# Gathering a tile's two entries one by one instead of together, in a four-layer graph kernel

## The chip, the cores and the metric

The kernel runs on one core of one Trainium2 chip. Its time is device time in microseconds (us) of one execution, as the median of the runs shown. The core has five engines, each with its own stream of instructions: TensorE (PE; its weight loads stand as PEld), VectorE (DVE), ScalarE (ACT), GpSimd (POOL) and SyncE (SP). [...]

## The reference

There are 16 entries. Each has 1024 nodes with 64 features and a dense adjacency of 1024 x 1024. Four layers follow each other, each added to its input and normalised over the features:

```
x = layernorm(x + gnn0(x, adj))     # two small matmuls on [x, adj @ x], tanh between them
x = layernorm(x + adj @ x / degree)
x = layernorm(x + quantile_gnn(x, adj, W1, b1, W2, b2))
x = layernorm(x + quantile_gnn(x, adj, W1', b1', W2', b2'))

def quantile_gnn(x, adj, ...):
    # drop some neighbours by their rank, keep the diagonal: the same set for both layers
    # per node and feature: sort the features of the neighbours that are left
    # agg = 0.25 * q(0.25) + 0.5 * q(0.5) + 0.25 * q(0.75), with linear interpolation
    return relu((x + agg) @ W1 + b1) @ W2 + b2
```

The last two layers cost the most: for each of 16 x 1024 nodes, and for each of 64 features, some 8 to 33 values are sorted, and that twice.

## The kernel before

**Tiles.** In each entry the nodes are ordered by their number of neighbours and cut into eight tiles of 128 nodes. The seven tiles of nodes with fewest neighbours (t = 0 to 6) have lists of 10, 11, 13, 14, 15, 17 and 19 slots (`SIZES`). Slot 0 is the node itself, the other slots hold its neighbours. The eighth tile is treated apart: TensorE picks its rows with one-hot matrices (`fill`, L762).

**Rounds.** Two entries, 2p and 2p + 1, are sorted together, as member m = 0 and m = 1 of a pair. A round is one pair in one of the two quantile layers. `order_of_rounds` (L953) alternates the layers after two rounds of the first; the first round of all has its two members sorted one after the other instead of together. `tasks` (L957) lists all tiles of all rounds, from t = 6 down to t = 0 in each.

**The ring.** The neighbours' rows come from tables in DRAM (six for each layer, one entry in each, L352) into a ring in SBUF, `got_s` (L1070): 60 slots (`ROOM`) for each of the two members. `fetch` (L977) gives a task the next free slots. For each member it has ScalarE copy slot 0 (L997), and GpSimd gather one slot after the other with an indirect DMA (L378, called at L999): one gather fetches one row of 64 floats for each of 128 nodes. A gather needs three things: the list of rows (`idx`, made by VectorE at the end of `lists`, L502), the table (written at L495 for the first layer, and at L888 by eight indirect DMAs for the second), and the slot free of its earlier user.

Tiles 6, 5 and 4 take 19 + 17 + 15 = 51 of the 60 slots. Tile 3 needs 14 and doesn't fit behind them, so it begins again at slot 0, once tile 6 is through.

**The sort.** `sort_round` (L1022) calls `fetch(n)` for each task, sorts by pairwise minimum and maximum on VectorE (`exchange`, L1014), and leaves the weighting of the sorted slots to `weigh` (L811), on ScalarE (L829) and VectorE. While a task's comparisons are written, `fetch()` is called after each one, and looks ahead.

**The order of the work.** All other work of the kernel (layers 0 and 1, lists, matmuls behind the sort, the eighth tile) consists of Python generators that `Weave` (L908) interleaves with the sorts. It decides by the estimated VectorE time that has been written so far. For VectorE, ScalarE and TensorE this written order is the order in which they run, because L1065 sets `manual_schedule` for these three. GpSimd and SyncE aren't in that list: the order of their streams is decided afterwards by the tile framework's scheduler, which puts each instruction where it finds it ready. So `fetch` fixes what a gather depends on and where slot 0's copy stands on ScalarE, and the scheduler fixes where the gather stands on GpSimd.

**SyncE** loads adjacency blocks (L433), writes the first layer's tables (L495) and reads the second layer's features back from DRAM (`read_back`, L902). `ready(b)` (L973) tells that an entry's lists and first-layer features have been written.

Of the kernel before, what the change touches and what calls it, by code (L numbers as in the profile page):

```python
# [25 lines left out]
SIZES = (10, 11, 13, 14, 15, 17, 19, 21, 33)  # L26
# [3 lines left out]
LINKS = [sum(SIZES[:t]) - t for t in range(LISTED + 1)]  # L30
KW = max(SIZES)
WIDE = max(2 * max(SIZES[:LISTED]), KW)
TABLES = 6
HOTS = 6
ROOM = 60
# [181 lines left out]
def adj_resnorm_kernel(ctx: ExitStack, tc: tile.TileContext, x, adj_t, nodemask, w01, b01, w02, b02,  # L217
                       w21, b21, w22, b22, w31, b31, w32, b32, out):
    nc = tc.nc
# [102 lines left out]
    for t, want in enumerate(wants):  # L322
        for first, m, stride, length in regular_runs(want):
            for r in range(m):
                k = first + r * stride
# [26 lines left out]
    table = [[dram.tile([N + 1, C], F32, name=f"table{layer}{i}") for i in range(TABLES)] for layer in range(2)]  # L352
# [24 lines left out]
    def gather(dst, tab, rows):  # L377
        nc.gpsimd.indirect_dma_start(out=dst, out_offset=None, in_=tab,  # L378
                                     in_offset=bass.IndirectOffsetOnAxis(ap=rows, axis=0))
# [377 lines left out]
    def members(k):  # L757

        layer, pair = order_of_rounds[k]
        return layer, [(m, 2 * pair + m, entries[2 * pair + m]) for m in range(2)]  # L760
# [188 lines left out]
    weave = Weave()  # L949
    tails = {}  # L950
    free, gots, room, holders = set(), [], [0], [None] * ROOM
    allowed = [1]
    order_of_rounds = [(0, 0), (0, 1)]  # L953
    for pair in range(2, B // 2):
        order_of_rounds += [(1, pair - 2), (0, pair)]
# [1 line left out]
    tasks = []  # L957
# [15 lines left out]
    def ready(b):  # L973

        return entries[b].listed and entries[b].xs[0] is not None

    def fetch(must=-1):  # L977

        while len(gots) < len(tasks):
            n = len(gots)  # L980
            k, t, present = tasks[n]
            layer, both = members(k)
            first = room[0] if room[0] + SIZES[t] <= ROOM else 0
            taken = [i for i in holders[first : first + SIZES[t]] if i is not None and tasks[i] not in free]
            there = [e.xs[1] is not None if layer else ready(b) for m, b, e in both if m in present]
            if n > must and (taken or not all(there)):
                return
            assert not taken
            holders[first : first + SIZES[t]] = [n] * SIZES[t]
            room[0] = first + SIZES[t]  # L990
            got = ring[:, :, first : first + SIZES[t], :]
            for m, b, e in both:
                if m not in present:
                    continue
                while not (e.xs[1] is not None if layer else ready(b)):
                    weave.advance()
                nc.scalar.copy(got[:, m, 0, :], e.xs[layer][:, t, :])  # L997
                for i in range(1, SIZES[t]):
                    gather(got[:, m, i, :], table[layer][b % TABLES], e.idx[:, LINKS[t] + i - 1 : LINKS[t] + i])  # L999
            gots.append(got)  # L1000

    def finish_round(k, agg, sums):
        for gen in sums:
# [10 lines left out]
    def exchange(t, pair, view):  # L1014

        for is_max, d, v, i, j, to in usual[t]:
            dve.tensor_tensor(view(pair[to], v, d if is_max else 0), view(pair[i], v), view(pair[j], v, d),
                              op=ALU.max if is_max else ALU.min)
            weave.catch_up()
            fetch()  # L1020

    def sort_round(k):  # L1022
# [13 lines left out]
        for n, (_, t, present) in enumerate(tasks):  # L1036
            if tasks[n][0] != k:
                continue
            fetch(n)
            got = gots[n]  # L1040
            which = slice(present[0], present[-1] + 1)
            count = len(present)
            other = s.lists.tile([P, WIDE, C], F32, name="other", bufs=1)
            other = other[:, : count * SIZES[t], :].rearrange("p (e s) c -> p e s c", e=count)
            exchange(t, (got[:, which], other), cut_pair)
            summed(t, got, which, present)
# [11 lines left out]
    with ExitStack() as main:  # L1058
# [11 lines left out]
        ring = s.lists.tile([P, 2, ROOM, C], F32, name="got_s")  # L1070
# [294 lines left out]
```

## Time and profile before

| what | value |
|---|---|
| time, median of 3 runs | 5304.49 us (5294.7 to 5307.4) |
| the profiled execution, its own time | 5293.2 us |
| span of that execution, first to last instruction | 5291.5 us |
| mean granted TensorE clock | 0.745 of full speed |

| engine | busy us | share of the span | instructions |
|---|---|---|---|
| PE (matmul) | 3412.4 | 64% | 43576 |
| DVE | 4296.5 | 81% | 9266 |
| ACT | 2809.6 | 53% | 6314 |
| POOL | 3467.3 | 66% | 3296 |

How to read it: a group of instructions is told by its line, engine, operation and tiles (what is written <- what is read), how many there were, their busy time, the mean duration of one in ns, and the idle time of the engine just before them with what ended most of it. "issue" is time in which an engine waited for nothing that the profile shows. [...]

### The profile page before, as it was taken

How to read it: one execution, taken by the hardware profiler on the slowest of the kernel's cores; microseconds unless marked ns; L12 is line 12 of the kernel's file. 1: busy time of each engine (PE TensorE's matmuls, PEld its weight loads, DVE VectorE, ACT ScalarE, POOL GpSimd, SP SyncE). 2: the span in 40 equal slices, each digit the busy share in tenths (PEclk: the TensorE clock that was granted, in tenths of full speed). 3: DMA queues.
4: the chain of work that ended last, by engine and by line, in shares of the span. 5: the costliest groups of instructions: out<-in, count | busy, mean ns of one | idle time of the engine just before them, and what ended most of it. 6: DMA issues, size and time to landing. Idle time of an engine off the chain costs nothing. (4 is left out here: it accounts for less than half of the span.)

```text
span 5291.5 us, 109614 instructions
## 1 busy us (share of the span) xinstructions
PE 3412.4 (64%) x43576; PEld 2637.1 (50%) x43576; DVE 4296.5 (81%) x9266; ACT 2809.6 (53%) x6314; POOL 3467.3 (66%) x3296
## 2 busy tenths in 40 slices
PE   6887886385765786766686775777769563424152
PEld 5656665263553665555564553655557352324141
DVE  2577848798788989897987987799899999596775
ACT  3566465466564665737383663738475653323242
POOL 0435327757477776767677674776767777777771
PEclk7888786697877787878687786877878775555555
DMA  2212212122222222221212122221212111111110
GB/s 84 79 50 72 65 39 59 46 52 53 52 54 52 59 62 57 57 57 45 70 43 57 50 48 53 57 59 50 60 51 58 25 28 26 26 24 27 26 24 7
DMA packets 420618, 259.31 MB, mean 49 GB/s; under 512 B 106603, under 2 KB 368891, under 8 KB 420091
## 3 DMA queue, kind: packets, MB, share of 16 engines
q1 hardware_dynamic: 317690, 147.12, 9.7%
q0 software_dynamic: 102400, 105.06, 9.4%
q8 instruction: 343, 5.62, 0.4%
q14 instruction: 185, 1.51, 0.1%
HBM read 239.37 MB, written 12.59 MB: 48 GB/s over the span
## 5 line engine op out<-in xcount | busy, mean ns | idle before, releaser
L378 POOL DMA_INDIRECT got_s<-table,idx x2944 | 3172.8, 1078 | 1634.3 <-issue 594.8
L374 PEld LDWEIGHTS <-hot 128*128 128x128 bf16 x24576 | 960.1, 108 | 1024.5 <-DVE hot L211 704.3
L374 PE MATMUL pgk<-x3p,hot 128*128 128x64 bf16 x12288 | 540.1, 210 | 469.6 <-DVE hot L211 402.9
L211 DVE TENSOR_TENSOR other<-got_s 128x512 f32<-128x512 f32 (+9 forms) x850 | 508.2, 609 | 390.7 <-DMA got_s<-table,idx 363.2
L374 PE MATMUL pgk<-x2p,hot 128*128 128x64 bf16 x12288 | 517.5, 207 | 321.2 <-DVE hot L211 258.9
L780 ACT COPY got<-pgk 64x256 f32<-64x256 f32 x416 | 151.9, 365 | 670.3 <-PE pgk L374 667.0
L211 DVE TENSOR_TENSOR got_s<-got_s 128x128 f32<-128x128 f32 (+9 forms) x867 | 481.9, 559 | 19.5 <-ACT got_s L829 1.7
L536 PE MATMUL pr<-steps,near 128*128 128x512 bf16 x1536 | 412.7, 429 | 131.6 <-ACT junk L542 83.5
L481 PE MATMUL pa<-x,adj_r 128*128 128x65 f32 x2048 | 387.6, 372 | 135.0 <-ACT x L404 58.1
L628 PE MATMUL pk<-near,order 128*128 128x512 f16 x2048 | 466.5, 381 | 3.9 <-DVE order L211 3.8
L829 ACT ACTIVATE got_s<-got_s,wts 128x64 f32<-128x64 f32 x1568 | 396.7, 336 | 135.4 <-DVE got_s L211 129.4
L481 PEld LDWEIGHTS pa<-x,adj_r 128*128 128x128 f32 x2048 | 377.2, 287 | 142.8 <-ACT x L404 60.1
L211 DVE TENSOR_TENSOR got_s<-other 128x512 f32<-128x512 f32 (+9 forms) x731 | 402.0, 563 | 7.5
L211 DVE TENSOR_SCALAR hot<-place 128x1024 bf16<-128x1024 f16 x768 | 329.1, 434 | 56.5 <-PE pgk L374 56.5
L211 DVE TENSOR_TENSOR other<-other 128x384 f32<-128x384 f32 (+10 forms) x617 | 323.7, 525 | 17.3
L536 PEld LDWEIGHTS <-near 128*128 128x128 f16 x1536 | 161.5, 108 | 351.8 <-issue 225.8
L211 DVE MAX8 best<-code 128x8 f16<-128x1024 f16 x240 | 293.8, 1224 | 45.9 <-ACT code L639 40.8
L628 PEld LDWEIGHTS <-order 128*128 128x128 bf16 x2048 | 193.9, 98 | 232.6 <-issue 11.6
L542 ACT ACTIVATE junk<-pr,nb_st 128x1024 f16<-128x1024 f32 x256 | 281.9, 1106 | 35.6 <-PE pr L536 34.9
L790 ACT ACTIVATE hot<-far,one_f 128x1024 bf16<-128x1024 f16 x256 | 294.0, 1148 | 8.4
L788 ACT ACTIVATE far<-place,minus_k 128x1024 f16<-128x1024 f16 x256 | 292.8, 1144 | 6.2 <-DVE place L211 4.4
L580 PE MATMUL pv<-minus_n,takes 128*128 128x128 bf16 x1024 | 209.5, 239 | 132.6 <-DVE takes L211 132.1
(205 smaller groups left out, 6727.9 us busy)
## 6 DMA issues: line engine op xcount, KB each, us to landing
adj_r<-in_adj_dram SPq DMA_DIRECT2D x256, 512.0 KB
got_s<-table,idx POOLq DMA_INDIRECT x2944
x_s<-in_x_dram SPq DMA_DIRECT2D x16, 256.0 KB
table<-x SPq DMA_DIRECT2D x16, 256.0 KB
x<-table SPq DMA_DIRECT2D x16, 256.0 KB
table<-x3s,rows POOLq DMA_INDIRECT x128
out_dram<-agg,out_rows POOLq DMA_INDIRECT x128
table<-no_row SPq DMA_DIRECT2D x12, 0.2 KB
```

Source lines behind the costliest of these rows:

```text
L211: return call(*args, **kwargs)
L374: nc.tensor.matmul(dst, hot[:, c, :], parts[:, c, q, :], start=first and c + q == 0, stop=c == NT - 1 and q == 2)
L378: nc.gpsimd.indirect_dma_start(out=dst, out_offset=None, in_=tab, in_offset=bass.IndirectOffsetOnAxis(ap=rows, axis=0))
L481: nc.tensor.matmul(pa[:, q, :], adj[i][:, jt, :], x1[:, jt, :], start=jt == 0, stop=jt == NT - 1)
L536: nc.tensor.matmul(pr[:, h * HALF : (h + 1) * HALF], near[:, c, t * P : (t + 1) * P], steps[:, ONSET + h * HALF - c * P :][:, :HALF], star ...
L542: nc.scalar.activation(junk, prs[t - 1], AF.Sign, bias=lim[:, i, t - 1 : t], scale=-1.0, accum_out=cut_at[:, i, t - 1 : t])
L580: nc.tensor.matmul(pv[:, cols], takes[:, c, rows], minus_n, start=False, stop=False)
L628: nc.tensor.matmul(cols, order[:, c, t * P : (t + 1) * P], left(c, slice(h * G, (h + 1) * G)), start=c == 0, stop=c == NT - 1)
L780: nc.scalar.copy(got[rows, off + waiting[0] : off + waiting[0] + 4, :], waiting[1][rows])
L788: nc.scalar.activation(far, e.place, AF.Abs, bias=minus_k[:, i + 2 : i + 3])
L790: nc.scalar.activation(by_act, far, AF.Relu, bias=one_f, scale=-1.0)
L829: nc.scalar.activation(got[:, m, i, :], got[:, m, slot_id, :], AF.Copy, scale=e.wts[:, t, i : i + 1])
```

## The change

`fetch` keeps one place for each member (`fetched`) in the list of tasks, in place of one for both. A new function, `fetch_one`, handles one member of one task. Member 0 may go ahead of member 1; member 1 may not pass member 0. The member that comes to a task first takes the ring slots for both. Before, a task was begun only once both members' lists had been written and the slots were free; after, each member begins once its own lists have been written and the slots are free. What is gathered, into which slots and from which lists, stays the same, and so do the copies of slot 0.

```diff
-    allowed = [1]
+    allowed, fetched = [1], [0, 0]
...
     def fetch(must=-1):
 
-        while len(gots) < len(tasks):
-            n = len(gots)
-            k, t, present = tasks[n]
+        moved = True
+        while moved:
+            moved = False
+            for m in range(2):
+                n = fetched[m]
+                if n < len(tasks) and (m == 0 or n <= fetched[0]):
+                    moved = fetch_one(n, m, must) or moved
+
+    def fetch_one(n, m, must):
+
+        k, t, present = tasks[n]
+        if m in present:
             layer, both = members(k)
-            first = room[0] if room[0] + SIZES[t] <= ROOM else 0
-            taken = [i for i in holders[first : first + SIZES[t]] if i is not None and tasks[i] not in free]
-            there = [e.xs[1] is not None if layer else ready(b) for m, b, e in both if m in present]
-            if n > must and (taken or not all(there)):
-                return
-            assert not taken
-            holders[first : first + SIZES[t]] = [n] * SIZES[t]
-            room[0] = first + SIZES[t]
-            got = ring[:, :, first : first + SIZES[t], :]
-            for m, b, e in both:
-                if m not in present:
-                    continue
-                while not (e.xs[1] is not None if layer else ready(b)):
-                    weave.advance()
-                nc.scalar.copy(got[:, m, 0, :], e.xs[layer][:, t, :])
-                for i in range(1, SIZES[t]):
-                    gather(got[:, m, i, :], table[layer][b % TABLES], e.idx[:, LINKS[t] + i - 1 : LINKS[t] + i])
-            gots.append(got)
+            _, b, e = both[m]
+
+            def there():
+                return e.xs[1] is not None if layer else ready(b)
+
+            if n > must and not there():
+                return False
+            if n == len(gots):
+                first = room[0] if room[0] + SIZES[t] <= ROOM else 0
+                if any(i is not None and tasks[i] not in free for i in holders[first : first + SIZES[t]]):
+                    assert n > must
+                    return False
+                holders[first : first + SIZES[t]] = [n] * SIZES[t]
+                room[0] = first + SIZES[t]
+                gots.append(ring[:, :, first : first + SIZES[t], :])
+            while not there():
+                weave.advance()
+            got = gots[n]
+            nc.scalar.copy(got[:, m, 0, :], e.xs[layer][:, t, :])
+            for i in range(1, SIZES[t]):
+                gather(got[:, m, i, :], table[layer][b % TABLES], e.idx[:, LINKS[t] + i - 1 : LINKS[t] + i])
+        elif n >= len(gots):
+            return False
+        fetched[m] = n + 1
+        return True
```

## The prediction

> **What bounds the kernel now.** I read the page's busy times and costliest groups first, then the waits of each engine, then GpSimd's work around one start of a round. From the page:
>
> ```profile
> PE 3412.4 (64%) x43576; PEld 2637.1 (50%) x43576; DVE 4296.5 (81%) x9266; ACT 2809.6 (53%) x6314; POOL 3467.3 (66%) x3296
> L378 POOL DMA_INDIRECT got_s<-table,idx x2944 | 3172.8, 1078 | 1634.3 <-issue 594.8
> ```
>
> VectorE is the bound: 4296.5 of 5291.5 us, in a stream that runs in written order. The other 995 us are waits or start-up. GpSimd is second, with 2944 gathers. From the views of the waits of VectorE, GpSimd and ScalarE:
>
> ```profile
> DVE other L211 <- DMA got_s<-table,idx: 363.2, 29, 26.4
> ...
> DVE other L211 <- ACT got_s L997: 9.8, 4, 5.2
> ```
> ```profile
> POOL got_s L378 <- DVE idx L211: 305.4, 6, 177.3
> ...
> POOL got_s L378 <- DVE y_x L211: 125.0, 5, 123.8
> ```
> ```profile
> ACT got_s L997 <- DVE agg L211: 23.8, 4, 12.7
> ```
>
> (Total, times, longest.) The largest single wait of VectorE is for gathers, 363.2 us in 29 pieces, and GpSimd stood idle 305.4 us for lists. So gathers that start earlier would be worth something. The question is whether the change makes them start earlier.
>
> The start of the second round (entries 2 and 3) answers it. GpSimd's timeline there:
>
> ```profile
> 568.56 1.00 POOL L378 DMA_INDIRECT got_s<-table,idx  x1 [43.34 <-DVE idx L211]
> ...
> 630.46 0.94 POOL L378 DMA_INDIRECT got_s<-table,idx  x1 [0.30 <-issue]
> 755.16 0.95 POOL L378 DMA_INDIRECT got_s<-table,idx  x1 [123.75 <-DVE y_x L211]
> ```
>
> and the instructions on the ring in three stretches (length; then DVE, ACT, POOL busy, with counts):
>
> ```profile
> 568.00:630.00 62.00, 0.00 (x0) 0.00 (x0) 47.42 (x47) 0.73 0.34 84
> 631.50:755.00 123.50, 0.00 (x0) 0.23 (x1) 0.00 (x0) 0.85 0.09 27
> 755.00:816.00 61.00, 15.62 (x24) 0.81 (x5) 47.13 (x46) 0.89 0.24 61
> ```
>
> From 568.56 to 630.46 a gather starts every 1.25 us, which makes 48. One member's share of tiles 6, 5 and 4 is 18 + 16 + 14 = 48, all that fits in the ring. Then GpSimd stops for 123.75 us, until the next member has its table and lists. The order of the two built programs, which holds no times, names the tables; both have:
>
> ```
> L378 DMACopy got_s<-table02 (entry 2) x48
> L378 DMACopy got_s<-table03 (entry 3) x48
> ```
>
> So member 0 is already gathered alone, before member 1's lists exist, in the kernel before. Python writes these gathers late, but GpSimd's stream isn't in written order: the scheduler moves each gather forward to where its inputs are ready. The wait for "both" that the change takes away stands in the Python code and not on the chip.
>
> **What the Trainium skill says.** "Perfetto Trace Analysis", section "Sequencer Loop": an engine's instructions are queued in order, and each waits for its own semaphores. So only a changed place in a stream, or a changed semaphore, can change the time, and I count these two. "DMA: Bandwidth & Descriptors", section "Anatomy of one DMA — SWDGE (gpsimd) path": a wait for a semaphore happens on the issuing sequencer before dispatch, not in the DMA engines. The trace agrees: the idle 123.75 us stand in front of the gather on GpSimd. "Perfetto Trace Analysis", section "DMA Instruction — SWDGE (GPSIMD)": the end shown is that of descriptor generation. I therefore price a gather by its spacing, 1.25 us in the timeline above (0.94 and 0.30 idle), not by its mean of 1.078.
>
> **The change part by part.** I compared the two built programs, instruction by instruction and wait by wait.
>
> 1. *VectorE and TensorE: the same instructions in the same order.* Two VectorE instructions name other gathers in their waits (part 4). Cost 0, and the engine that bounds the kernel keeps its stream.
>
> 2. *ScalarE: 18 of 224 copies of slot 0 move forward.* They are member 0's copies for tiles 6, 5 and 4, in seven rounds (3, 3, 3, 3, 2, 1 and 3). One takes 0.240 us by the median of its row, so 18 x 0.240 = 4.3 us arrive at earlier places, at most 3 x 0.24 = 0.7 us at each start of a round, and leave later ones. What is behind them there is ordinary ScalarE work (L820, L829, L780, L788, L636 and the like) on an engine that is busy 53%. Net 0. Bounds: +4.3 us if VectorE waited for every one of them, -4.3 us if it waits for every one now. I take 0: of VectorE's 9.8 us for these copies, 5.2 fall at 1433.6, where five copies run in a burst and VectorE starts behind the first, which belongs to member 1 and doesn't move.
>
>    *A new wait in front of them?* A copy that moved forward could meet its slot still in use and hold everything behind it on ScalarE: the weighting of L829, and the one-hot matrices of L788 and L790 for which TensorE waits. Seventeen of the 18 carry no wait at all in either program, because ScalarE has by then waited for something later. One has gained a wait, for a VectorE comparison that ended at 2505.4 in this trace. Its new neighbours on ScalarE ran at 2518.3, so it is 13 us late for that. Cost 0; if the cover went, the longest wait that any of these copies had is 12.7 us.
>
> 3. *GpSimd, near 1957 us: one table write goes behind eight gathers.* The eight scatters of entry 5's rows (L888) stand together before; after, the eighth stands behind eight gathers of entry 6. It is delayed by 8 x 1.27 = 10 us, and these gathers come one place earlier, 1.3 us. SyncE's read-back (L902) waits for that scatter, and one adjacency load (L433) that stood behind the read-back now stands before it:
>
> ```profile
> 1932.84 8.63 SPq L433 DMA_DIRECT2D adj_r<-in_adj_dram  x3
> 1958.86 0.37 SPq L902 DMA_DIRECT2D x<-table  x1
> 1959.32 68.30 SPq L433 DMA_DIRECT2D adj_r<-in_adj_dram  x4
> ```
>
>    The read-back moves from 1958.9 to about 1969. Its first reader, ScalarE's split at L410, runs at 2010.5 without having waited, so over 30 us of cover remain. The load behind goes out earlier, at about 1948; the next load waited 60.8 us for VectorE, until 2020.8, anyway. The gathers that come first are followed by the next member's at 1969.7, which waited for its lists. Cost 0; without any cover, +10 us.
>
> 4. *GpSimd, near 3150 us: two gathers of tile 5 (member 0) go ahead of tile 6's last (member 1).* The last gather of tile 6 moves back by two places, 2.5 us, from 3165.4. VectorE first reads the tile at 3268.9, so over 100 us of cover remain. Cost 0; without cover +2.5 us.
>
> All other GpSimd instructions keep their places: 21 of some 3200 indirect DMAs moved. Sum: 0, with bounds of -4.3 and 4.3 + 10 + 2.5 = +16.8 us if every cover failed at once. Against the profiled execution: span 5291.5, own time 5293.2 us, so again 5293 us. That execution lies 11 us under the median of the runs, and a change of nothing leaves the median at 5304.
>
> **The rivals.**
>
> - *Slower: slot 0's copies block ScalarE.* Place: the seven starts of rounds of part 2. Price: 12.7 us each, the longest wait that such a copy had. If VectorE came to need what is queued behind, 7 x 12.7 = 89 us: 5304 + 89 = 5393. It decides from the point at which VectorE's last use of the slot ends later than ScalarE arrives. For it: ScalarE runs in order, and VectorE depends on it. Against it: 17 of the 18 have no wait, and the 18th has 13 us of margin. 4 in 100, with all other slower outcomes.
> - *Faster: member 0's gathers do start earlier.* GpSimd's idle time for lists, less the first 177.3 us in which no list exists, is 305.4 - 177.3 = 128 us. If all of it were filled with useful gathers, and VectorE were freed of as much out of its 363.2: 5304 - 128 = 5176. For it: both waits are real. Against it: the 48 gathers stand in front of the second member's already, and the ring has no room for a 49th. 4 in 100, with a gain by a luckier interleaving.
> - *The delayed read-back is seen.* VectorE's layer work for a later entry slips by the 10 us: 5314. That is 0.2%, still within no change. 2 in 100.
> - *No change,* 5304: 90 in 100.
>
> **How the numbers follow.** About 0.3% (16 us) is what a measurement of this kernel can tell from no change; four executions of the kernel before lie between 5293.2 and 5307.4. The likeliest case gives 5304. For the range, the scatter counts more than any part: about 12 us below, which takes in the -4.3 of part 2 and the fastest executions, and some 9 above, of which 4.3 are part 2 and the rest is scatter. That is 5292 to 5313, nine tenths of the chance; the two far cases stay outside. Faster 0.04, the same 0.90 + 0.02 = 0.92, slower 0.04.
>
> **What would show it.** Right: VectorE's wait for gathers stays near 363 us and GpSimd's for lists near 305; at the second round's start GpSimd again makes 48 gathers from about 568 and stops for about 124 us; L997's copies wait no longer than some 30 us in total; busy times stay within a few us. Wrong: a new wait of tens of us at L997 on ScalarE followed by VectorE's waits for L829 or L780 (the slower rival), or gathers of a second member with nothing idle before them and VectorE's 363 us markedly smaller (the faster one). The forecast also fails if small shifts change how the granted TensorE clock moves, which no part of the sum covers.

## The result, and the profile after

| kernel | time, median (lowest to highest) | executions |
|---|---|---|
| before | 5299.86 us (5294.7 to 5307.4) | 12 |
| after | 5304.02 us (5291.91 to 5308.1) | 12 |

The ratio after / before is 1.0005, with a 95% interval of 0.9996 to 1.0014: no change that can be measured. The profiled execution of after took 5306.79 us by its own time, with a clock of 0.743. From the page of the kernel after:

```profile
PE 3435.2 (65%) x43576; PEld 2659.3 (50%) x43576; DVE 4297.6 (81%) x9266; ACT 2809.1 (53%) x6314; POOL 3464.7 (65%) x3296
...
L378 POOL DMA_INDIRECT got_s<-table,idx x2944 | 3170.9, 1077 | 1650.7 <-issue 604.9
```

VectorE, ScalarE and GpSimd are busy for the same time as before, to 3 us each. The waits of VectorE, GpSimd and ScalarE in the kernel after (total, times, longest):

```profile
DVE other L211 <- DMA got_s<-table,idx: 352.9, 28, 26.4
...
DVE other L211 <- ACT got_s L1010: 9.8, 4, 5.2
```
```profile
POOL got_s L378 <- DVE idx L211: 310.9, 8, 179.5
POOL got_s L378 <- DVE other L211: 271.4, 103, 49.6
...
POOL got_s L378 <- DVE y_x L211: 126.4, 3, 125.8
```
```profile
ACT got_s L1010 <- DVE agg L211: 23.6, 5, 11.3
ACT got_s L1010 <- DVE got_s L211: 9.4, 5, 3.5
```

L1010 is what L997 was before. Of the waits that the prediction showed, none has moved by more than some 10 us; 352.9 against 363.2 us is the largest difference. GpSimd's timeline at the start of the second round, in the kernel after:

```profile
580.79 1.01 POOL L378 DMA_INDIRECT got_s<-table,idx  x1 [43.92 <-DVE idx L211]
...
642.65 0.94 POOL L378 DMA_INDIRECT got_s<-table,idx  x1 [0.30 <-issue]
769.40 0.94 POOL L378 DMA_INDIRECT got_s<-table,idx  x1 [125.81 <-DVE y_x L211]
```

and the ring's instructions in three stretches of it (length; then DVE, ACT, POOL busy):

```profile
580.00:643.00 63.00, 0.00 (x0) 0.52 (x3) 47.88 (x48) 0.70 0.34 83
643.00:769.00 126.00, 0.00 (x0) 0.00 (x0) 0.59 (x1) 0.84 0.10 27
```

It is the picture of before, again 48 gathers and then a stop of 126 us. (The prediction's "every 1.25 us" is the commonest spacing. From the first of the 48 starts to the last it is 61.9 us in both kernels, 1.32 us from one to the next on the mean. So the 48 rests on the count and not on the spacing.) Only ScalarE has changed in it: its three copies of member 0 now run in the first stretch (612.0 to 612.3; 664.0 and later before).

Everything here stands some 12 us later than in the kernel before. That isn't the change: the first gather already starts at 188.2 instead of 186.0, and the second entry's first gather at 389.4 instead of 377.0, ahead of the first instruction that the change moves. The span of this execution is 13 us longer (5304.9 against 5291.5 us), so hardly more is added after that.

One thing is needed to read the experiments: on two of the four chips that they ran on, every kernel, the one before too, took some 7250 to 7800 us instead of 5180 to 5650, so each is compared only with the kernel before on its own chip.

### The profile page after: what moved, and what is told of

Its sections match the earlier page's. It is cut to its first block, busy times and chain, and to the rows that moved or that the text cites. A ratio compares the mean times of both kernels' runs of the same rounds, so it can differ in the third digit from the quotient of the medians.

```text
span 5304.9 us, 109613 instructions
## 1 busy us (share of the span) xinstructions
PE 3435.2 (65%) x43576; PEld 2659.3 (50%) x43576; DVE 4297.6 (81%) x9266; ACT 2809.1 (53%) x6314; POOL 3464.7 (65%) x3296
## 5 line engine op out<-in xcount | busy, mean ns | idle before, releaser
L374 PEld LDWEIGHTS <-hot 128*128 128x128 bf16 x24576 | 972.2, 109 | 1011.9 <-DVE hot L211 696.7
L211 DVE TENSOR_TENSOR other<-got_s 128x512 f32<-128x512 f32 (+9 forms) x850 | 508.7, 609 | 387.4 <-DMA got_s<-table,idx 352.9
L450 PE MATMUL px<-adj_r,x_s 128*64 128x128 f32 x2048 | 287.9, 302 | 13.6 <-ACT node_in L453 9.2
```

Of the source, the lines that this page charges most:

```text
L211: return call(*args, **kwargs)
L374: nc.tensor.matmul(dst, hot[:, c, :], parts[:, c, q, :], start=first and c + q == 0, stop=c == NT - 1 and q == 2)
L450: nc.tensor.matmul(px[C:, q * P : (q + 1) * P], x_s[:, jt, :], adj[t][:, jt, :], start=jt == 0, stop=jt == NT - 1)
```

## The experiments

**1. What is "both when both are ready" worth, if the chip follows it?** The prediction said that the chip never did: the scheduler starts a member's gathers as soon as their own inputs are there. This was tried with two kernels made from the kernel before. In the first, VectorE copies a member's whole list onto itself at the end of `lists`, and every gather of this member then waits for that copy:

```diff
         e.listed = True
+        if b > 1:
+            nc.vector.tensor_copy(e.idx, e.idx)
...
             for m, b, e in both:
+                while m in present and not (e.xs[1] is not None if layer else ready(b)):
+                    weave.advance()
+            for m, b, e in both:
                 if m not in present:
                     continue
-                while not (e.xs[1] is not None if layer else ready(b)):
-                    weave.advance()
```

In the second, the copies of both members are made when the second list is ready, so that on the chip neither member can start without the other's list:

```diff
-        if b > 1:
-            nc.vector.tensor_copy(e.idx, e.idx)
+        if b > 1 and b % 2:
+            for other in (entries[b - 1], e):
+                nc.vector.tensor_copy(other.idx, other.idx)
```

They have the same instructions; on VectorE, TensorE and ScalarE only the places of the 14 list copies differ. Each pair ran on two chips. What was expected:

> The kernel before, with one small VectorE copy of each entry's list onto itself (14 in all, entries 2 to 15) at the end of that entry's lists, so that its gathers wait for this copy. It is the control for the next run. Theory (the scheduler already gathers each member alone; only real dependencies count): the same as before within 0.3%, since 14 copies of about 0.2 us are 3 us; at the second round's start again 48 gathers, a stop of about 124 us, 48 gathers. Rival (member 0's gathers are worth 128 us if they come early, and something holds them back on the chip): the same too.

> As the control, but both copies of a pair stand at the end of the later member's lists, so that member 0's gathers really wait on the chip until both lists are there: what the Python code of the kernel before seems to say. Theory: member 0's 48 gathers (60 us) move behind the stop, so that GpSimd's idle time for lists grows by some 60 us in each round in which the later lists come late; VectorE feels little of it, because with 1.25 us a gather tile 6 of both members would be ready at 755 + 45 = 800 where VectorE began at 793, at 1382 + 45 = 1427 before 1434, at 1970 + 45 = 2015 before 2021, and in later rounds with more room: 10 us slower (0.2%), up to 40 if the later tiles feel the backlog. Rival 1 (being early is worth all of the 128 us of idle time): 128 us slower than the control, 2.4%. Rival 2 (the kernel before gates on the chip already): the same as the control, with the same picture on GpSimd.

> The control once more, since in its first look every kernel, the one before too, took some 7300 us with TensorE waiting for nothing that the profile shows, so that the bound was another than in the case. Theory: the same as before within 0.3% where the kernel before takes some 5300 us.

> The gate once more, for the same reason. Theory: 10 us slower than its control (0.2%), up to 40; GpSimd makes no gather of member 0 before the stop at the second round's start. Rival (being early is worth all of the 128 us of idle time): 128 us slower, 2.4%.

| kernel | median us | before on the same chip | ratio (95% interval) |
|---|---|---|---|
| own list, second chip | 5394.86 | 5299.27 | 1.0182 (1.0155 to 1.0209) |
| both lists, second chip | 5651.68 | 5299.27 | 1.066 (1.0638 to 1.0681) |
| own list, first chip | 7256.36 | 7340.5 | 0.9893 (0.9853 to 0.9932) |
| both lists, first chip | 7447.21 | 7340.5 | 1.0154 (1.01 to 1.0208) |

On the second chip, waiting for both lists costs 5651.68 - 5394.86 = 257 us over waiting for one's own. On the first, where the time is another, it is 7447.21 - 7256.36 = 191 us. Both theories missed: the own-list kernel isn't within 0.3% of before on either chip, and the gate costs neither 10 to 40 us nor the 128 us of the rival. The second chip's profiles show how. VectorE's wait for gathers in the kernel that waits for its own list:

```profile
DVE other L211 <- DMA got_s<-table,idx: 413.9, 31, 27.9
```

and in the one that waits for both:

```profile
DVE other L211 <- DMA got_s<-table,idx: 677.9, 44, 47.6
```

VectorE's wait for gathers grows by 677.9 - 413.9 = 264 us, and the span by 5642.1 - 5382.6 = 259.5 us. So this one wait accounts for all of it. GpSimd's timelines in the same second round show where it begins. Own list:

```profile
603.28 1.33 POOL L378 DMA_INDIRECT got_s<-table,idx  x1 [77.58 <-DVE other L211]
...
794.32 0.94 POOL L378 DMA_INDIRECT got_s<-table,idx  x1 [123.13 <-ACT got_s L1000]
```

Both lists:

```profile
794.26 0.94 POOL L378 DMA_INDIRECT got_s<-table,idx  x1 [268.12 <-DVE idx L654]
```

With its own list, member 0 starts at 603 and member 1 at 794, with 48 gathers each. With both lists, all 96 start at 794, member 0's 191 us later than in the other kernel, and the stop in front of them, 268.12 us, is put down to the list copy (L654). VectorE feels it at once. Its first comparison of this round, on tile 6 of both members, with its own list and then with both:

```profile
819.19 0.56 DVE L211 TENSOR_TENSOR other<-got_s 128x384 f32<-128x384 f32 x1 [25.61 <-DMA got_s<-table,idx]
```
```profile
841.69 0.56 DVE L211 TENSOR_TENSOR other<-got_s 128x384 f32<-128x384 f32 x1 [47.58 <-DMA got_s<-table,idx]
```

In the kernel before it ran at 793.38, with 0.17 us of waiting. The theory of 10 us had put the late start at 755, where member 1's gathers start in the kernel before; the copy of the whole list makes it 794.

The second kernel is what the words of the change describe as "before". The kernel before doesn't look like it: in its trace member 0 starts at 568.56.

The first kernel shows something finer. It waits for nothing but its own whole list, and is still 95.6 us (1.8%) slower than the kernel before. `lists` writes `idx` tile by tile, tile 6 first, and the gathers of tile 6 depend only on the columns that they read. So the chip starts them before the list is complete, ahead of `listed` and so of `ready(b)`, for which the code of both kernels waits. The first and the last columns of entry 2's list, as VectorE writes them in the kernel before:

```profile
568.12 0.17 DVE L211 TENSOR_SCALAR idx<-best 128x18 int32<-128x18 f16 x1
601.99 0.17 DVE L211 TENSOR_SCALAR idx<-best 128x9 int32<-128x9 f16 x1
```

GpSimd starts at 568.56, right behind the first. With the copy it starts at 603.28, behind the last. Of the 91 us by which the span is longer, 413.9 - 363.2 = 51 us are VectorE's wait for gathers. Another 35 us are VectorE's waits in front of `other` comparisons for nothing that the profile shows (37.9 against 3.1 us), so for these the later gathers aren't shown to be the cause. On the first chip the same edit took 1.1% off; why a later start of the gathers is no loss there, the runs don't say.

**2. Is it the scheduler that makes the two kernels the same?** Each gather was chained to the one written before it, in the kernel before and in the kernel after, so that GpSimd issues them in written order:

```diff
-                    gather(got[:, m, i, :], table[layer][b % TABLES], e.idx[:, LINKS[t] + i - 1 : LINKS[t] + i])
+                    with tc.issue_after(chain[-1].ins) if chain else ExitStack():
+                        chain.append(gather(got[:, m, i, :], table[layer][b % TABLES], e.idx[:, LINKS[t] + i - 1 : LINKS[t] + i]))
```

> The kernel before, with every gather of the sorted tiles put behind the one written before it (an order of issue only, no wait for its end), so that GpSimd gathers in the order of the Python code. Theory: the order on GpSimd is the scheduler's work, so that here the code's order shows for the first time: at the second round's start 18 gathers of member 0, then the stop of about 60 + 124 us, then the rest. Slower than before by 10 us as in the gate, and by what an order that can't step aside for a free slot costs within the rounds: 0 to 100 us. Rival (the order of the code was GpSimd's order all the time): the same as before.

> The changed kernel with the same chain. Theory: now the change acts on GpSimd: 48 gathers of member 0, the stop of about 124 us, 48 of member 1, and this is 5 to 40 us faster than the chained kernel before (0.1 to 0.8%). Rival (the change does nothing wherever GpSimd's order comes from): the two chained kernels are the same, in the time and on GpSimd. Rival (early gathers are worth 128 us): 128 us faster than the chained kernel before.

> The kernel before with its gathers chained in the order of the Python code, once more where the kernel before takes some 5300 us. Theory, with what the gate showed (early gathers are worth more than I had put): at the second round's start 18 gathers of member 0, a stop for member 1's lists, then the rest; slower than before by 100 to 400 us, most of it from the rounds, where a gather can't step aside for a slot that is free. Rival (the order of the code was GpSimd's order all the time): the same as before.

> The changed kernel with the same chain. Theory: 48 gathers of member 0, the stop, 48 of member 1, and 10 to 100 us faster than the chained kernel before, less than the 257 us that the gate cost over its control, since here member 1's lists are waited for tile by tile. Rival (the change does nothing wherever GpSimd's order comes from): the two chained kernels are the same.

In the built programs the two now differ as the diff reads: in the second round GpSimd issues 18, 18, 16, 16, 14 and 14 gathers, members in turn, for the chained kernel before, and 48 and 48 for the chained kernel after. The traces show it too. GpSimd's first gather of the second round and the first one behind the stop, in the chained kernel before (second pair):

```profile
783.86 1.01 POOL L378 DMA_INDIRECT got_s<-table,idx  x1 [56.78 <-DVE idx L211]
...
989.92 0.94 POOL L378 DMA_INDIRECT got_s<-table,idx  x1 [183.80 <-DVE y_x L211]
```

and in the chained kernel after:

```profile
770.89 1.00 POOL L378 DMA_INDIRECT got_s<-table,idx  x1 [56.66 <-DVE idx L211]
...
1010.16 0.95 POOL L378 DMA_INDIRECT got_s<-table,idx  x1 [179.47 <-DVE y_x L211]
```

Between the two lines stand 18 gathers in the one and 48 in the other, counted with the first. So once GpSimd follows the written order, the change does on the chip what it says: it lets member 0 go ahead of member 1's lists. It is the scheduler that makes the two kernels alike without the chain.

Both pairs ran on chips where the kernel before took about 7300 us:

| pair | chained before | chained after | their ratios to before |
|---|---|---|---|
| first | 7782.58 us | 7779.88 us | 1.061 (1.0561 to 1.0659) and 1.0593 (1.0547 to 1.0639) |
| second | 7783.24 us | 7738.86 us | 1.0583 (1.0538 to 1.0628) and 1.0522 (1.0466 to 1.0578) |

The intervals overlap in both pairs, so what the change is worth in time without the scheduler isn't settled there: the forecasts of 5 to 40 us and of 10 to 100 us are neither met nor refuted by 2.7 and 44 us. The chain itself costs 5 to 6% on those chips, in both kernels. For the kernel before it is 442 and 421 us, far above the first expectation (some 100 us at most) and a little above the second (400 us, meant for a chip of 5300 us). Where that cost arises isn't shown; VectorE's wait for gathers is too small for it. At 5300 us the pair wasn't run. The profiles say why these chips answer the question badly. From VectorE's waits of the chained kernel after:

```profile
DVE other L211 <- DMA got_s<-table,idx: 51.0, 8, 10.5
```

VectorE hardly waits for gathers there (51.0 us, and 79.1 in the chained kernel before, against 352.9 in the kernel after at 5300 us), so starting them earlier can give little.

**3. Is the place of slot 0's copies on ScalarE free?** The copy was written twice in the kernel after, which makes 224 more of them:

```diff
             nc.scalar.copy(got[:, m, 0, :], e.xs[layer][:, t, :])
+            nc.scalar.copy(got[:, m, 0, :], e.xs[layer][:, t, :])
```

> The changed kernel with each copy of a finding entry's list into its ring place written twice (224 more copies on ScalarE, 224 x 0.240 us = 54 us more of its busy time; nothing is left out). Theory (part 2 of the prediction: these copies stand ahead of their gathers with time to spare, so where they stand on ScalarE is free): within 0.3% of the kernel before, 5285 to 5315 us, VectorE's wait for gathers near 350 us as in the changed kernel. Rival (ScalarE is close to the path at these places, the change escaped by luck): up to the full 54 us, 5340 to 5360 us. If the kernel before itself takes about 7300 us on this chip, TensorE's issue binds and the run says little: within 0.5% either way.

It took 5301.47 us (5293.62 to 5305.81), against 5298.15 us for the kernel before on the same chip: ratio 1.0, interval 0.9991 to 1.0009. The page of this kernel shows that the work was added:

```profile
PE 3392.4 (64%) x43512; PEld 2627.1 (50%) x43576; DVE 4297.0 (81%) x9266; ACT 2863.4 (54%) x6538; POOL 3467.3 (66%) x3296
```

ScalarE is busy for 2863.4 - 2809.1 = 54 us more, and the time stays. So the 0.24 us that a copy takes is free at all 224 places, in time that can be measured. The run doesn't price the other danger of part 2, a copy that blocks what stands behind it: a second copy to the same slot finds it free. That is answered by the kernel after itself, in which these copies wait hardly longer in total than before (33 and 31 us, see part 2 below).

**4. Does the ring hold the early gathers back?** In the second round member 0 stops after 48 gathers because tile 3 has no room behind tiles 6, 5 and 4. With 68 places it has, in a round that starts at place 0 (51 + 14 = 65). To fit in SBUF, the one-hot matrices `hot` of the eighth tile get four buffers instead of six. A run with the four buffers alone stands beside it:

```diff
-HOTS = 6
-ROOM = 60
+HOTS = 4
+ROOM = 68
```

> The changed kernel with four buffers for the one-hot matrices in place of six, which frees 4 KB in each partition. It is the control for the next run. Theory: 0 to 80 us slower (up to 1.5%), as TensorE's picks wait for VectorE's one-hot matrices already (704 us).

> The same with a ring of 68 slots in place of 60, so that tile 3 fits behind tiles 6, 5 and 4 (65 slots) and 61 gathers of a member can go ahead. Theory (the depth of the ring, not the rule for who may begin, limits how early gathers are): VectorE's wait for gathers falls from 353 us to 150 to 300, and the time lies 50 to 200 us under the control. Rival (GpSimd's rate of 1.25 us a gather limits it): the wait and the time stay within 20 us of the control.

> The changed kernel with four hot matrices in the place of more and a ring of 68 places in the place of 60 (nothing is left out). Theory (the gathers that a member's own lists release early are held by ring places that the member before still uses, not by the lists): VectorE's wait for gathers falls from about 350 us by 30 us or more, and the time is 0.3 to 1% under the kernel before. Rival (the lists, not the ring, hold the gathers): no change of that wait by more than 10 us, time within 0.5% or up to 80 us longer for the hot matrices. If the kernel before takes about 7300 us on this chip, the run says nothing on it, as with the earlier pair.

| kernel | median us | before on the same chip | ratio (95% interval) |
|---|---|---|---|
| four `hot` buffers | 7280.6 | 7362.27 | 0.9882 (0.9845 to 0.992) |
| four `hot` buffers, 68 places | 7286.95 | 7362.27 | 0.9885 (0.9834 to 0.9937) |
| four `hot` buffers, 68 places, other chip | 5181.85 | 5298.15 | 0.9776 (0.9755 to 0.9796) |

At 7300 us the two can't be told apart, and both are 1.2% faster than before, where the four buffers were expected to cost up to 1.5%; the runs don't say why. At 5300 us the kernel with both settings saves 5298.15 - 5181.85 = 116 us, 2.2%, more than the 0.3 to 1% that the theory gave it; it is faster than both kernels of this study. Its waits of VectorE:

```profile
DVE hot L211 <- PE pgk L374: 201.0, 112, 7.2
DVE other L211 <- DMA got_s<-table,idx: 135.7, 11, 29.9
```

and of GpSimd:

```profile
POOL got_s L378 <- DVE other L211: 145.0, 105, 44.6
```

Against the kernel after, VectorE's wait for gathers falls from 352.9 to 135.7 us, where the theory said by 30 us or more. GpSimd's wait for comparisons that still use a ring place (`other`) falls from 271.4 to 145.0 us. GpSimd's timeline at the start of the second round in this kernel:

```profile
568.67 1.00 POOL L378 DMA_INDIRECT got_s<-table,idx  x1 [45.86 <-DVE idx L211]
...
645.91 0.94 POOL L378 DMA_INDIRECT got_s<-table,idx  x1 [0.30 <-issue]
758.12 0.94 POOL L378 DMA_INDIRECT got_s<-table,idx  x1 [111.27 <-DVE y_x L211]
```

From the first line to the second GpSimd makes 59 gathers instead of 48, and the stop that follows is 111 instead of 126 us. The stop itself stays, since member 1's table and lists are no earlier.

The expected 61 gathers were wrong for this round. The trace gives only the count, but the rule by which `fetch` gives out places says why. With 60 places the lists of a round end at place 48, and the next tile 6 needs 19 more, so every round begins at place 0 and places 51 to 59 are never used. With 68 places the start moves (0 and 34 for the two members of the first round, 21 for the second round, then 0, 34, 21 again), and 65 places are used. In the second round tiles 6, 5 and 4 take places 21 to 39, 40 to 56 and 0 to 14, and tile 3 begins at 15 and runs into tile 6. What can go ahead is 48 gathers, five of tile 3 (places 16 to 20) and six of tile 0 (places 57 to 62), together 59. The same working gives 48 for the ring of 60. So the ring of 60 works as one of 51, and the ring of 68 as one of 65.

The price shows as well: `hot` now waits 201.0 us for TensorE to release a buffer, 60.0 in the kernel after. The four buffers alone weren't run at 5300 us, nor was the deeper ring with the code of the kernel before, so neither the share of each setting nor whether the change helps the deeper ring is measured. That the ring brings the gain, and the buffers only the cost, is read from the waits and not shown by a run.

## Why the prediction was right

**The mechanism.** The prediction's first statement, that the wait for both stands in the Python code and not on the chip, is shown from three sides. The kernel after has the second round that the kernel before has. A kernel in which the wait does stand on the chip looks different (one stop of 268 us) and is 257 us slower than its control: between these two, taking the wait away brings 257 of 5651.68 us, 4.5%. And with GpSimd held to the written order, the two kernels do differ on the chip, 18 gathers against 48. The change brought nothing because the scheduler's order had already taken that wait away, and more: the gathers start before a member's list is complete.

**Part 1** (VectorE and TensorE, 0): VectorE's busy time is 4297.6 against 4296.5 us, and its waits for gathers differ by 10 us.

**Part 2** (18 copies on ScalarE, 0): that the copies' own time is free is shown by experiment 3, that they block nothing by the waits of the kernel after. L1010's waits total 23.6 + 9.4 = 33 us, where the prediction said some 30; before, the same two rows were 23.8 and 7.6 us. The copies near the gained wait ran at 2523.4 and 2531.1 and are not preceded by any wait.

**Part 3** (a table write behind eight gathers, 0): the move is there. GpSimd and then SyncE in the kernel after:

```profile
1976.98 0.95 POOL L378 DMA_INDIRECT got_s<-table,idx  x1 [0.30 <-issue]
1978.23 1.00 POOL L888 DMA_INDIRECT table<-x3s,rows  x1 [0.30 <-issue]
```
```profile
1943.74 16.54 SPq L433 DMA_DIRECT2D adj_r<-in_adj_dram  x4
1980.48 0.37 SPq L902 DMA_DIRECT2D x<-table  x1
```

Four adjacency loads instead of three now stand ahead of the read-back, which goes out at 1980.48 instead of 1958.86. Of these 21.6 us some 12 are the scatter of this execution, which leaves 10, as worked out. The split at L410 ran at 2021.7 instead of 2010.5, later by the same scatter and no more, so 41 us of cover were left, where "over 30" was claimed.

**Part 4** (two gathers ahead of tile 6's last, 0): VectorE first reads the tile at 3280.5 instead of 3268.9, again 12 us later like everything else, and without a wait. The move was not tried by itself.

**The rivals.** ScalarE blocked by slot 0's copies: no wait of tens of us has come at L1010. Member 0 starting earlier by the change: it doesn't. The price of 128 us was made from the idle time that GpSimd still has in the kernel before, and that is what is left when the scheduler has done its part. So it is no price for the wait that the words of the change describe. In the kernel that waits for both, GpSimd stands idle for lists much longer:

```profile
POOL got_s L378 <- DVE idx L654: 450.4, 3, 268.1
POOL got_s L378 <- DVE idx L211: 222.8, 5, 178.1
```

That is 673 us. In its control it is 368 us, and 491 with a stop of 123.1 us that is put down to slot 0's copy but ends at the list copy (793.6). The difference, 182 us, is above the 128 too; why VectorE loses still more, 264 us, isn't worked out. The sentence set against this rival, that the ring has no room for a 49th gather, named a limit that does hold: with more room 59 gathers go ahead, and the kernel, with four `hot` buffers, takes 5182 us. That this lies near the rival's 5176 is chance. GpSimd's waits for lists and tables, which the rival wanted to fill, are no shorter there (333.6 and 111.9 us, against 310.9 and 126.4). The delayed read-back was not seen (part 3).

**The sizes.** The forecast of 5304 was the median of the three timed runs then known; twelve give 5299.86 for before and 5304.02 for after. The scatter was the main part of the range, and it was the main part of what came.

## What to carry to other kernels

A condition in the code that writes a kernel is not a wait on the chip: before pricing its removal, see in the trace, or in the order of the built streams, whether the chip ever waits there, above all on an engine whose order a scheduler chooses. When an early start seems to be worth something and doesn't come, ask what the buffer allows, and count the places that it really uses: here a ring of 68 places uses 65, where the ring of 60 uses 51, and with it came a gain that earlier permission didn't bring. A cheap test of a suspected gate is to make it real and see what it costs.

## What the runs showed of the hardware

The same program took about 5300 us on two of the four chips of the experiments and about 7300 us on the other two. The kernel that waits for its own list has a profile on one chip of each kind. VectorE is busy for 4313.2 us on the first chip and 4298.1 on the second, nearly the same, while the time is 7256.36 and 5394.86 us. The waits of TensorE's weight loads show a difference. First chip, then second:

```profile
PEld L374 <- issue: 1639.7, 1379, 25.7
```
```profile
PEld L374 <- issue: 266.4, 213, 6.0
```

TensorE stood for 1640 instead of 266 us in front of these loads without waiting for anything that the profile shows. Its mean granted clock was 0.673 instead of 0.742. VectorE then waits for it: 389.5 instead of 56.7 us for TensorE to release a buffer of `hot`, to name one wait. The cause is open. The prediction counted changed places and changed semaphores alone; here the same program takes some 1900 us more, so such a count holds for one chip at a time.

It decides what a change is worth. Where TensorE holds VectorE up like this, VectorE finds most of its gathers landed (it waits 38.1 us for them instead of 413.9). Waiting for one's own list costs 1.8% on the second chip and gains 1.1% on the first, and the deeper ring, worth 116 us together with its four buffers at 5300 us, can't be told from its control at 7300 us. But not everything is hidden: waiting for both lists instead of one costs 191 us there too.
